# Three output units' rows of x gathered a stage earlier, PSUM tiles split by row half, and mask set-up moved into stage 1

## The chip, the cores and the metric

One core of one Trainium2 chip runs the whole program. The metric is the device time of one execution in microseconds (us), and less is better. Times "before" are the median of three runs. The profile is of one further execution, with a time of its own. In profile lines PE is the tensor engine, PEld its weight load, DVE the vector engine, ACT the scalar engine, POOL the GpSimd engine and SP the sync engine, which here only issues transfers. "SPq" and "POOLq" mark an engine's own issue queue.

## The reference, cut to what matters

Two layers act on x, an array of 512 x 512 positions with 64 channels, in float32. Each adds to x a function of the group-normed x.

```
# layer 0, on xn = layernorm(groupnorm(x)); m = sequence_mask (512 values of 0 or 1)
left  = (xn @ left_w  + left_b)  * m_i * m_j * sigmoid(xn @ lgate_w + lgate_b)
right = (xn @ right_w + right_b) * m_i * m_j * sigmoid(xn @ rgate_w + rgate_b)
out   = einsum('bkjd,bkid->bijd', left, right)            # per channel, sum over k
x1    = x + (layernorm(out) @ out_w + out_b) * sigmoid(xn @ ogate_w + ogate_b)
# layer 1: 12 x 12 low Fourier modes of groupnorm(x1), mixed by complex weights, transformed back
result = x1 + real(ifft2(mixed modes))
```

Rows and columns whose mask is 0 add nothing to `out`. About half of the mask is 1, and when at most 256 (K) of the 512 are, the kernel takes the path `compact`, which packs the masked rows and columns into 256 "slots". That path runs here.

## The kernel before, in words

`compact` is one stream of instructions per engine. Its stages are written out by hand, so each engine works in program order and an instruction that waits holds up everything behind it on its engine.

**Stage 1** (to about 200 us): 16 column blocks `jc` (L677). For each, POOL gathers four tiles of 1 MB from x (`fetch_tile`, L664; the gather itself is L638), PE transposes them (L687), DVE takes statistics of the transposes (`bn_stats`, L688, sixteen per block) and ACT and POOL copy the masked columns of two of the tiles into `xc`, a tile of 257 slots that fills 128.5 KB of each partition (`keep`, L670). After block 8 `make_weights` (L171) scales and centres the weights: short DVE steps, each waiting for a PE product. At the end `group_norm_affine` gives `ab1` (L701), which stage 2 needs.

**Stage 2, the slots' stage** (to about 440 us): iterations q = -14 to 63, one group of four slots each (L773). A group is transposed to channels in place (L719), centred and squared 13 iterations before its use (L727), and its row factors are spread over partitions by way of DRAM in packs of four groups (`spread`, L744: a store `rs_d` and two loads `rbc`, all on POOL's queue, 1 MB together). For q >= 0 `normed` (L759) scales the group, `project` (L764) makes gates and sides in PSUM, ACT takes the sigmoid of the gates into `sigc` (L778), DVE joins both into `o_c` (L795) and SP stores the halves to `left_d` and `right_d` (L807), 512 KB per iteration. From q = 51 on there is no group left to centre, and only the projection half of the loop body runs. `gates_c`, `sides_c` and `sigc` are single buffers that hold both row halves r = 0, 1.

**Between stages 2 and 3** (L813 to L853): broadcast rows of two biases, `center_x` and `gate_x`, the tile `places` (128 KB per partition, used as scratch by everything later), the target indices `dst_i`, and the slots' masks `mask_s` and `mask_own`.

**Stage 3** (to about 621 us): per channel, `left` and `right` are loaded (L865), transposed and multiplied (L895), masked (L900) and stored to `tri_d` (L903).

**Stage 4** (to about 1470 us): a loop over pieces `s` (L1193), eight to a step; 8 steps for the packed product, then 32 for the units of the output, one unit each. The first part makes `u_d`: `load_product` (L1022) brings a product pair into a ring of four buffers, one transfer per partition half; PE multiplies it (L1058), ACT squares and copies (L1078, L1079), DVE reduces and scales (L1083, L1271), POOL adds a bias (L1278) and SP stores `u_d` (L1283). From s = -LEAD on, PE and ACT run 12 to 13 pieces ahead of DVE and POOL. A unit of the output is a pair (column block, half of the rows). `load` (L1091) gathers its two 1 MB tiles of x into one of five ring places of `places`, three units ahead of its use (L1241); so the six gathers of units 0 to 2 stand in the last three steps of the `u_d` part. Then come the gate (L1045), the sigmoid (L1221), the product and the sum with x on POOL (L1109, L1113), statistics and Fourier sums, and the store to `x1_h`.

**Stage 5** (to the end): rows come back from `x1_h`, the inverse transform is added (L1447), and the result is stored (L1448).

Of the kernel before, what the change touches and what calls it, by code (L numbers as in the profile page):

```python
# [9 lines left out]
F32 = mybir.dt.float32  # L10
I32 = mybir.dt.int32
AF = mybir.ActivationFunctionType
ALU = mybir.AluOpType
# [33 lines left out]
def conv_preact_kernel(ctx: ExitStack, tc: tile.TileContext, t: dict):  # L47
# [573 lines left out]
    def compact(fc):  # L621
# [29 lines left out]
            return regs  # L651


        with tc.tile_pool(name="xc", bufs=1) as cp:
            xc = cp.tile([P, K + 1, 2, C], F32, name="xc")
            with tc.tile_pool(name="f1", bufs=1) as sp, tc.tile_pool(name="f1x", bufs=2) as xp, tc.tile_pool(
                name="f1y", bufs=4
            ) as yp, tc.tile_pool(name="f1p", bufs=6, space=PSUM) as pt, tc.manual_schedule():
                make_weights = load_weights(sp, nc.sync)
                sets = chunk_sets(fc, 4, 1)  # L660
                quarter = NJ // 4
                xgs = {}

                def fetch_tile(jc):  # L664
                    xg = xp.tile([P, 2, JC, C], F32, name="xg")
                    xgs[jc] = xg, [xg[:, 0], xg[:, 1]] + [yp.tile([P, JC, C], F32, name="yg") for _ in range(2)]
                    for r, part in enumerate(xgs[jc][1]):
                        gather(part.rearrange("p j c -> p (j c)"), tiles, src_i, r, jc)

                def keep(engine, copy, jc, first, last):  # L670

                    for j, slot in enumerate(slots_of(engine, jc, first, last), first):
                        copy(xc[:, bass.ds(slot, 1)].rearrange("p o r c -> p (o r) c"), xgs[jc][0][:, :, j, :])  # L673

                fetch_tile(0)
                fetch_tile(1)
                for jc in range(NJ):  # L677
                    if jc % quarter == 0:
                        stats = sp.tile([P, 1, 16 * quarter, 6], F32, name="stats1c")
                    for r in range(4):  # L680
                        flat = xgs[jc][1][r].rearrange("p j c -> p (j c)")
                        for c in range(4):

                            ps = pt.tile([P, 4, P], F32, name="x_ps")
                            for i in range(4):
                                o = (8 * c + 2 * i) * C
                                nc.tensor.transpose(ps[:, i, :], flat[:, o : o + P], ident)  # L687
                            nc.vector.bn_stats(  # L688
                                stats[:, 0, 16 * (jc % quarter) + 4 * r + c, :], ps.rearrange("p i k -> p (i k)")
                            )  # L690
# [14 lines left out]
            with tc.tile_pool(name="fn", bufs=2) as np_, tc.tile_pool(name="fw", bufs=2) as wk, tc.tile_pool(  # L705
# [56 lines left out]
                    nc.vector.tensor_mul(xns[q], gts(q), rbs[k][:, n])  # L762

                def project(q, k):  # L764
                    ps = pp.tile([P, 2, N], F32, name=k + "_c")
                    for r in range(2):
                        h = slice(r * C, (r + 1) * C)
                        nc.tensor.matmul(ps[:, r, :], weights[k][h], xns[q][h], start=True, stop=True)
                    return ps


                lead = QB + 9
                for q in range(-lead - 1, groups):  # L773
                    live = lambda i: 0 <= q + i < groups
                    if live(0):
                        gates = project(q, "gates")
                        sig = sp.tile([P, 2, N], F32, name="sigc")
                        nc.scalar.activation(sig, gates, AF.Sigmoid, bias=biases["gates"])  # L778
                    if live(1):
                        normed(q + 1)  # L780
                    for step in todo[:3]:
# [3 lines left out]
                        channels(q + lead + 1)  # L785
                    if live(lead - QB) and (q + lead - QB) % QB == QB - 1:
                        spread((q + lead - QB) // QB)
                    if live(lead):
                        sq, total = centered(q + lead)
                    if live(0):  # L790
# [2 lines left out]
                        res = op.tile([P, 4, 2, P], F32, name="o_c")  # L793
                        for r in range(2):
                            nc.vector.scalar_tensor_tensor(  # L795
                                res[:, :, r, :], sides[:, r].rearrange("p (i k) -> p i k", i=4), biases["sides"],
                                sig[:, r].rearrange("p (i k) -> p i k", i=4), ALU.add, ALU.mult,
                            )
                    if live(lead):
                        nc.vector.tensor_reduce(  # L800
# [9 lines left out]
                            )  # L810


        rows_of = {}  # L813
        with tc.tile_pool(name="rb", bufs=2) as rp, tc.tile_pool(name="rbp", bufs=2, space=PSUM) as rps:
            for name in ("ogate", "out"):
                wide = rp.tile([P, P], F32, name="wide_" + name, tag="wide")
                nc.vector.tensor_copy(wide, biases[name].to_broadcast([P, P]))
                ps = rps.tile([P, C], F32, name="row_" + name, tag="row")
                nc.tensor.matmul(ps, wide, ident[:, :C], start=True, stop=True)
                rows_of[name] = fc.tile([P, C], F32, name="bias_row_" + name)  # L820
                nc.vector.tensor_copy(rows_of[name], ps)
        nc.gpsimd.dma_start(u_d[:, K, 0, :], rows_of["out"])
        nc.gpsimd.dma_start(u_d[:, K, 1, :], rows_of["out"])

        center_x = fc.tile([P, P], F32, name="center_x")
        gate_x = fc.tile([P, P], F32, name="gate_x")
        nc.vector.tensor_scalar(center_x, center, ab1[:, 0:1], None, ALU.mult)
        nc.vector.tensor_scalar(gate_x, weights["ogate"], ab1[:, 0:1], None, ALU.mult)


        with tc.tile_pool(name="tri", bufs=1) as trp:

            places = trp.tile([P, K * 2 * C], F32, name="places")

            dst_i = fc.tile([P, 4, NJ // 2], I32, name="dst_i")
            base = fc.tile([P, 4], F32, name="dst_base")
            nc.vector.tensor_scalar(base, rank_p, float(NJ // 2), None, ALU.mult)
            for b in range(4):
                nc.vector.tensor_scalar(dst_i[:, b, :], few_i, base[:, b : b + 1], None, ALU.add)
            mask_s = fc.tile([P, K], F32, name="mask_s")  # L840
            mask_own = fc.tile([P, 2], F32, name="mask_own")
            with tc.tile_pool(name="mk", bufs=1) as mk, tc.tile_pool(name="mkp", bufs=1, space=PSUM) as mps:
                mask_ps = mps.tile([P, K], F32, name="mask_ps")
                for b in range(2):
                    wide = mk.tile([P, P], F32, name=f"wide{b}")
                    nc.vector.tensor_copy(wide, slot_t[:, b, 1:2].to_broadcast([P, P]))
                    nc.tensor.matmul(mask_ps[:, b * P : (b + 1) * P], wide, ident, start=True, stop=True)
                nc.vector.tensor_copy(mask_s, mask_ps)
                own = mk.tile([P, 2, P], F32, name="own")
                nc.vector.tensor_mul(  # L850
                    own, mask_s.rearrange("p (q b) -> p b q", b=2), ident.unsqueeze(1).to_broadcast([P, 2, P])
                )
                nc.vector.tensor_reduce(mask_own, own, AX.X, ALU.add)  # L853
# [65 lines left out]
            RING = 5  # L919
            first = K * 2 // 64  # L920

            units = [(jc, half) for jc in range(NJ) for half in ((1, 0) if jc < NJ - 1 else (0, 1))]
            total_g = (first + len(units)) * SIZE
            with tc.manual_schedule(), tc.tile_pool(name="late", bufs=1) as lp:
                sets = chunk_sets(lp, 8)
# [9 lines left out]
                sums = lp.tile([P, MODES, M2], F32, name="sums")  # L935
                nc.vector.memset(sums, 0.0)


                order = (0, 1, 3, 4, 2)
# [50 lines left out]
                with tc.tile_pool(name="np_x", bufs=LEAD + 2) as tp, tc.tile_pool(name="np_q", bufs=2) as sqp, tc.tile_pool(  # L990
# [30 lines left out]

                    def load_product(q):  # L1022

                        for h in range(2):
                            nc.sync.dma_start(
                                products_t[q % 4][h * C : (h + 1) * C],
                                tri_d.rearrange("c j i -> c (j i)")[:, (2 * q + h) * 2 * N : (2 * q + h + 1) * 2 * N],
                            )

                    def transpose(s):  # L1030
                        k, n = divmod(s, SIZE)
# [161 lines left out]
                    for s in range(-LEAD, total_g + 2 * SIZE):  # L1193
# [340 lines left out]
```

## Time and profile before

| | us |
|---|---|
| median of 3 runs | 1786.14 |
| lowest and highest run | 1781.57, 1787.03 |
| profiled execution, its own time | 1777.78 |
| span of that execution | 1776.0 |
| PE busy in the span | 1567.8 (88%) |
| DVE busy | 1413.7 (80%) |
| ACT busy | 933.0 (53%) |
| POOL busy | 936.5 (53%) |
| moved by DMA | 518.48 MB |

The span is what the profiler covers; 1.8 us of the execution's time lie around it. The profiled execution was faster than each of the three runs. A line of the timeline has the start in us, the duration, the engine, the program line, the operation, `result<-operands`, sizes and, in brackets, how long the engine had stood idle before it and what ended that. A line of the windows view has the stretch, its length, then busy time and instruction count of PE, PEld, DVE, ACT and POOL, the clock granted to PE (1.00 is full), the mean busy share of the 16 DMA engines and GB/s. A line of the waits view has engine and line, what it waited for, the total in us, how often, and the longest.

### The profile page before, as it was taken

The page shows a single profiled execution, that of the slowest core. Times are in us where ns is not written, and L with a number is a line of the kernel's source. Part 1 is how long each engine was busy: PE and PEld are TensorE (multiplying, and loading weights), DVE is VectorE, ACT ScalarE, POOL GpSimd, SP SyncE. Part 2 cuts the span into 40 slices and gives each one's busy share as a digit, 9 for nine tenths or more (in the row PEclk, how much of TensorE's full clock was granted, in tenths as well). Part 3 has the DMA queues.
Part 4 walks back from the last instruction along what each step waited for, and adds up shares of the span by engine and source line. Part 5 has one row for each costly group of instructions (what it writes and reads, how often), then busy time and mean ns, then how long its engine had stood idle before and what let it go on. Part 6 is the DMA issues. An engine that isn't in the chain of part 4 may idle for free. (4 is left out here: it accounts for less than half of the span.)

```text
span 1776.0 us, 32619 instructions
## 1 busy us (share of the span) xinstructions
PE 1567.8 (88%) x10918; PEld 1242.0 (70%) x10918; DVE 1413.7 (80%) x2982; ACT 933.0 (53%) x1660; POOL 936.5 (53%) x695
## 2 busy tenths in 40 slices
PE   6779799997999978899999999999999977998772
PEld 5667666662899867787888888888888745665341
DVE  7989678887455568688999999999999984865451
ACT  3666566663333266676777777777777742011000
POOL 4666211111000037698999999999999881111110
PEclk9999999999899999899999999999999976555555
DMA  7999278878898789868767767776776699999999
GB/s 281 386 386 388 107 206 227 229 229 245 279 305 303 257 246 347 298 196 296 265 242 257 253 233 259 264 249 239 249 264 244 212 318 400 425 427 427 426 427 385
DMA packets 192593, 518.48 MB, mean 292 GB/s; under 512 B 37664, under 2 KB 104480, under 8 KB 151456
## 3 DMA queue, kind: packets, MB, share of 16 engines
q1 hardware_dynamic: 156112, 295.65, 47.5%
q0 software_dynamic: 32832, 218.45, 33.4%
q10 hardware_dynamic: 3472, 2.20, 0.5%
q8 instruction: 89, 1.46, 0.3%
q14 instruction: 88, 0.72, 0.1%
HBM read 311.60 MB, written 204.60 MB: 291 GB/s over the span
## 5 line engine op out<-in xcount | busy, mean ns | idle before, releaser
L1045 PE MATMUL w_ps<-gate_x,xt_c 128*128 128x128 f32 x2048 | 280.5, 281 | 30.0 <-DVE z_t L1274 28.6
L1113 POOL TENSOR_TENSOR places<-places,z_t 128x1024 f32<-128x1024 f32 x127 | 301.3, 2372 | 8.0
L1045 PEld LDWEIGHTS w_ps<-gate_x,xt_c 128*128 128x128 f32 x2048 | 252.0, 194 | 46.4 <-DVE z_t L1274 44.6
L1045 PE MATMUL c_ps<-center_x,xt_c 128*128 128x128 f32 x2048 | 277.0, 279 | 0.8 <-ACT xt_c L1040 0.4
L1045 PEld LDWEIGHTS c_ps<-center_x,xt_c 128*128 128x128 f32 x2048 | 252.8, 194 | 3.8 <-ACT xt_c L1040 3.0
L1440 PE MATMUL l_ps<-places,rinv 24*128 24x512 f32 x512 | 206.2, 1118 | 29.3 <-DVE places L1447 19.0
L1168 DVE BATCH_NORM_STATS2 stats2c<-places 128x6 f32<-128x128 f32 x1024 | 220.5, 278 | 9.9 <-POOL places L1113 9.9
L1083 DVE TENSOR_REDUCE scratch<-sq_c 128x16 f32<-128x1024 f32 x160 | 194.6, 1216 | 31.1 <-ACT sq_c L1078 16.1
L1221 ACT ACTIVATE z_t<-z_t 128x1024 f32<-128x1024 f32 x128 | 135.5, 1058 | 131.8 <-DVE z_t L1280 131.1
L1440 PEld LDWEIGHTS l_ps<-places,rinv 24*128 24x128 f32 x512 | 119.8, 302 | 110.8 <-DVE places L1447 56.9
L1278 POOL TENSOR_TENSOR z_t<-z_t,bias_row_out 128x1024 f32<-128x1024 f32 x32 | 75.6, 2363 | 226.3 <-PE y_ps L1058 202.1
L1040 ACT ACTIVATE xt_c<-t_ps,ab_xc 128x512 f32<-128x512 f32 x256 | 176.0, 688 | 11.5 <-PE t_ps L1038 10.6
L1274 DVE TENSOR_TENSOR z_t<-w_ps,rs_n 128x512 f32<-128x512 f32 x256 | 172.0, 672 | 6.2 <-PE w_ps L1045 6.1
L1076 ACT ACTIVATE sq_c<-c_ps 128x512 f32<-128x512 f32 x256 | 150.8, 589 | 31.4 <-PE c_ps L1045 30.8
L1280 DVE TENSOR_TENSOR z_t<-z_t,scratch 128x1024 f32<-128x1024 f32 x128 | 156.3, 1221 | 9.9 <-ACT rs_n L1089 3.7
L688 DVE BATCH_NORM_STATS2 stats1c<-x_ps 128x6 f32<-128x512 f32 x256 | 157.1, 682 | 7.7 <-PE x_ps L687 7.4
L1109 POOL TENSOR_TENSOR z_t<-z_t,places 128x1024 f32<-128x1024 f32 x64 | 151.8, 2371 | 14.6 <-ACT z_t L1221 14.4
L1038 PE MATMUL t_ps<-c_ident,places 128*128 128x128 f32 x1024 | 158.4, 278 | 0.0
L1038 PEld LDWEIGHTS t_ps<-c_ident,places 128*128 128x128 f32 x1024 | 118.5, 142 | 51.4 <-issue 51.4
L1447 DVE TENSOR_TENSOR places<-places,l_ps 128x512 f32<-128x512 f32 x176 | 109.3, 682 | 55.2 <-DMA places<-x_h,dst_i 42.1
L1109 POOL TENSOR_TENSOR z_t<-z_t,bias_row_out 128x1024 f32<-128x1024 f32 x63 | 149.4, 2372 | 5.8 <-ACT z_t L1221 5.5
L673 ACT COPY xc<-xg 128x128 f32 x352 | 105.0, 298 | 66.1 <-POOL xc L673 47.1
(214 smaller groups left out, 2557.0 us busy)
## 6 DMA issues: line engine op xcount, KB each, us to landing
x_h<-places SPq DMA_DIRECT2D x64, 1024.0 KB
out_x<-places SPq DMA_DIRECT2D x44, 1024.0 KB
places<-u_d SPq DMA_DIRECT2D x512, 64.0 KB
out_x<-lx_t SPq DMA_DIRECT2D x20, 1024.0 KB
rbc<-rs_d POOLq DMA_DIRECT2D x32, 512.0 KB, 7.1
left_d<-o_c SPq DMA_DIRECT2D x64, 256.0 KB
right_d<-o_c SPq DMA_DIRECT2D x64, 256.0 KB
left_raw<-left_d SPq DMA_DIRECT2D x64, 256.0 KB
```

The source lines that it names most:

```text
L688: nc.vector.bn_stats(stats[:, 0, 16 * (jc % quarter) + 4 * r + c, :], ps.rearrange("p i k -> p (i k)"))
L1038: nc.tensor.transpose(tps[:, i, :], flat[:, o : o + P], ident)
L1040: nc.scalar.activation(xts[s], tps, AF.Identity, bias=ab1[:, 2:3])
L1045: nc.tensor.matmul(ps[:, 2 * i : 2 * i + 2, :], xts[s][:, i, :], w, start=True, stop=True)
L1076: nc.scalar.activation(sq, cps, AF.Square)
L1083: nc.vector.tensor_reduce(totals[k % 2][:, 8 * (n - 1) : 8 * (n + 1)], sqs.pop(s // 2), AX.X, ALU.add)
L1109: nc.gpsimd.tensor_mul(zs[k, c], zs[k, c], u)
L1113: nc.gpsimd.tensor_add(xr, xr, zs.pop((k, c)))
L1168: nc.vector.bn_stats(st[k // 4][:, g, k % 4, :], x_of(k)[:, :, 2 * g : 2 * g + 2])
L1274: nc.vector.tensor_mul(z[:, 8 * odd : 8 * odd + 8, :], wps, rs)
L1280: nc.vector.tensor_add(z, z, bias_ps["ogate"].unsqueeze(1).to_broadcast([P, 16, C]))
L1440: nc.tensor.matmul(ps.rearrange("p j o -> p (j o)"), rinv[h, b, :], it[h], start=True, stop=True, tile_position=(32 * g, 0),)
```

## The change

1. **Early gathers.** `xc` stays allocated after stage 2, and `places` becomes a view of its first 256 slots. In stage 2, at q = 34, 38, ... 54, `early` gathers the six tiles of x of units 0 to 2 into slots whose groups have been projected. Stage 4 starts its own gathers with unit 3.
2. **A PSUM tile per row half.** `project` makes two PSUM tiles, and the sigmoid two SBUF tiles from two activations of half the size. Matmuls and `o_c` steps are as many as before.
3. **Set-up in stage 1.** Bias rows, masks and `dst_i` are made by `prepare_rows` right after `make_weights`, in block 8 of stage 1. Its broadcast and product tiles share one buffer (the tag `scaled`, `bufs=1`). The product for `mask_own` is made in two halves. `center_x` and `gate_x` move into iteration q = -2 of stage 2.
4. **One transfer per product pair.** `load_product` issues one transfer of 128 partitions in place of two of 64.

```diff
+        xc = held.enter_context(tc.tile_pool(name="xc", bufs=1)).tile([P, K + 1, 2, C], F32, name="xc")
+        places = xc.rearrange("p s r c -> p (s r c)")[:, : K * 2 * C]
+        order = (0, 1, 3, 4, 2)
+        EARLY = 3
+        def early(i):
+            k, r = divmod(i, 2)
+            o = (order[k] * 2 + r) * JC * C
+            gather(places[:, o : o + JC * C], tiles, src_i, 2 * units[k][1] + r, units[k][0])
...
+        def prepare_rows(rp):
+            with tc.tile_pool(name="slp", bufs=2, space=PSUM) as rps:
+                for name in ("ogate", "out"):
+                    wide = rp.tile([P, P], F32, name="wide_" + name, tag="scaled")
+                    nc.vector.tensor_copy(wide, biases[name].to_broadcast([P, P]))
+                    ps = rps.tile([P, C], F32, name="row_" + name, tag="row")
+                    nc.tensor.matmul(ps, wide, ident[:, :C], start=True, stop=True)
+                    rows_of[name] = fc.tile([P, C], F32, name="bias_row_" + name)
+                    nc.vector.tensor_copy(rows_of[name], ps)
+                for r in range(2):
+                    nc.gpsimd.dma_start(u_d[:, K, r, :], rows_of["out"])
+                mask_ps = rps.tile([P, K], F32, name="mask_ps", tag="row")
+                for b in range(2):
+                    wide = rp.tile([P, P], F32, name=f"wide{b}", tag="scaled")
+                    nc.vector.tensor_copy(wide, slot_t[:, b, 1:2].to_broadcast([P, P]))
+                    nc.tensor.matmul(mask_ps[:, b * P : (b + 1) * P], wide, ident, start=True, stop=True)
+                nc.vector.tensor_copy(mask_s, mask_ps)
+                for b in range(2):
+                    own = rp.tile([P, P], F32, name=f"own{b}", tag="scaled")
+                    nc.vector.tensor_mul(own, mask_s.rearrange("p (q b) -> p b q", b=2)[:, b], ident)
+                    nc.vector.tensor_reduce(mask_own[:, b : b + 1], own, AX.X, ALU.add)
+                nc.vector.tensor_scalar(base, rank_p, float(NJ // 2), None, ALU.mult)
+                for b in range(4):
+                    nc.vector.tensor_scalar(dst_i[:, b, :], few_i, base[:, b : b + 1], None, ALU.add)
...
                     if jc == NJ // 2:
                         make_weights(fc, cp)
+                        prepare_rows(sp)
...
                 def project(q, k):
-                    ps = pp.tile([P, 2, N], F32, name=k + "_c")
-                    for r in range(2):
+                    made = [pp.tile([P, N], F32, name=f"{k}_c{r}") for r in range(2)]
+                    for r, ps in enumerate(made):
...
-                        sig = sp.tile([P, 2, N], F32, name="sigc")
-                        nc.scalar.activation(sig, gates, AF.Sigmoid, bias=biases["gates"])
+                        sigs = [sp.tile([P, N], F32, name=f"sigc{r}") for r in range(2)]
+                        for sig, ps in zip(sigs, gates):
+                            nc.scalar.activation(sig, ps, AF.Sigmoid, bias=biases["gates"])
...
+                    if q in range(34, 34 + 8 * EARLY, 4):
+                        early((q - 34) // 4)
+                    if q == -2:
+                        nc.vector.tensor_scalar(center_x, center, ab1[:, 0:1], None, ALU.mult)
+                        nc.vector.tensor_scalar(gate_x, weights["ogate"], ab1[:, 0:1], None, ALU.mult)
...
-        with tc.tile_pool(name="rb", bufs=2) as rp, tc.tile_pool(name="rbp", bufs=2, space=PSUM) as rps:
-            for name in ("ogate", "out"):
-                wide = rp.tile([P, P], F32, name="wide_" + name, tag="wide")
...
-            places = trp.tile([P, K * 2 * C], F32, name="places")
...
-                own = mk.tile([P, 2, P], F32, name="own")
...
-                nc.vector.tensor_reduce(mask_own, own, AX.X, ALU.add)
...
                     def load_product(q):
-                        for h in range(2):
-                            nc.sync.dma_start(
-                                products_t[q % 4][h * C : (h + 1) * C],
-                                tri_d.rearrange("c j i -> c (j i)")[:, (2 * q + h) * 2 * N : (2 * q + h + 1) * 2 * N],
-                            )
+                        nc.sync.dma_start(
+                            products_t[q % 4], tri_d.rearrange("c (q h j) i -> q h c (j i)", h=2, j=4)[q]
+                        )
...
-                        if 0 <= v + 3 < len(units):
+                        if EARLY <= v + 3 < len(units):
                             if n == 3:
                                 load(v + 3, 0)
```

More of the change, by code (lines that the diff above doesn't have):

```diff
@@ L651, in slots_of @@
             return regs
-        with tc.tile_pool(name="xc", bufs=1) as cp:
-            xc = cp.tile([P, K + 1, 2, C], F32, name="xc")
+        held = ExitStack()
+        xc = held.enter_context(tc.tile_pool(name="xc", bufs=1)).tile([P, K + 1, 2, C], F32, name="xc")
+        places = xc.rearrange("p s r c -> p (s r c)")[:, : K * 2 * C]
+        units = [(jc, half) for jc in range(NJ) for half in ((1, 0) if jc < NJ - 1 else (0, 1))]
+        order = (0, 1, 3, 4, 2)
[4 more added lines that the diff above has]
+            gather(places[:, o : o + JC * C], tiles, src_i, 2 * units[k][1] + r, units[k][0])
@@ new lines, in compact @@
+        rows_of = {}
+        mask_s = fc.tile([P, K], F32, name="mask_s")
+        mask_own = fc.tile([P, 2], F32, name="mask_own")
+        dst_i = fc.tile([P, 4, NJ // 2], I32, name="dst_i")
+        base = fc.tile([P, 4], F32, name="dst_base")
+        center_x = fc.tile([P, P], F32, name="center_x")
+        gate_x = fc.tile([P, P], F32, name="gate_x")
+        def prepare_rows(rp):
[22 more added lines that the diff above has]
+                    nc.vector.tensor_scalar(dst_i[:, b, :], few_i, base[:, b : b + 1], None, ALU.add)
@@ L656, in compact @@
+        with tc.tile_pool(name="wt", bufs=1) as cp:
             with tc.tile_pool(name="f1", bufs=1) as sp, tc.tile_pool(name="f1x", bufs=2) as xp, tc.tile_pool(
@@ L764, in project @@
                 def project(q, k):
-                    ps = pp.tile([P, 2, N], F32, name=k + "_c")
-                    for r in range(2):
+                    made = [pp.tile([P, N], F32, name=f"{k}_c{r}") for r in range(2)]
+                    for r, ps in enumerate(made):
                         h = slice(r * C, (r + 1) * C)
-                        nc.tensor.matmul(ps[:, r, :], weights[k][h], xns[q][h], start=True, stop=True)
-                    return ps
+                        nc.tensor.matmul(ps, weights[k][h], xns[q][h], start=True, stop=True)
+                    return made
                 lead = QB + 9
@@ L795, in compact @@
                             nc.vector.scalar_tensor_tensor(
-                                res[:, :, r, :], sides[:, r].rearrange("p (i k) -> p i k", i=4), biases["sides"],
-                                sig[:, r].rearrange("p (i k) -> p i k", i=4), ALU.add, ALU.mult,
+                                res[:, :, r, :], sides[r].rearrange("p (i k) -> p i k", i=4), biases["sides"],
+                                sigs[r].rearrange("p (i k) -> p i k", i=4), ALU.add, ALU.mult,
                             )
@@ L810, in compact @@
                             )
-        rows_of = {}
-        with tc.tile_pool(name="rb", bufs=2) as rp, tc.tile_pool(name="rbp", bufs=2, space=PSUM) as rps:
-            for name in ("ogate", "out"):
-                wide = rp.tile([P, P], F32, name="wide_" + name, tag="wide")
[L817 to L831, printed above, removed]
-            places = trp.tile([P, K * 2 * C], F32, name="places")
[L835 to L848, printed above, removed]
-                own = mk.tile([P, 2, P], F32, name="own")
-                nc.vector.tensor_mul(
-                    own, mask_s.rearrange("p (q b) -> p b q", b=2), ident.unsqueeze(1).to_broadcast([P, 2, P])
-                )
-                nc.vector.tensor_reduce(mask_own, own, AX.X, ALU.add)
@@ L854, in compact @@
+        with held:
             with tc.tile_pool(name="ti", bufs=5) as ip, tc.tile_pool(name="tt", bufs=3) as tp, tc.tile_pool(
@@ L920, in compact @@
             first = K * 2 // 64
-            units = [(jc, half) for jc in range(NJ) for half in ((1, 0) if jc < NJ - 1 else (0, 1))]
             total_g = (first + len(units)) * SIZE
@@ L936, in compact @@
                 nc.vector.memset(sums, 0.0)
-                order = (0, 1, 3, 4, 2)
                 def place(i):
@@ L1022, in load_product @@
                     def load_product(q):
-                        for h in range(2):
-                            nc.sync.dma_start(
-                                products_t[q % 4][h * C : (h + 1) * C],
-                                tri_d.rearrange("c j i -> c (j i)")[:, (2 * q + h) * 2 * N : (2 * q + h + 1) * 2 * N],
-                            )
+                        nc.sync.dma_start(
+                            products_t[q % 4], tri_d.rearrange("c (q h j) i -> q h c (j i)", h=2, j=4)[q]
+                        )
                     def transpose(s):
```

## Prediction

> **What bounds the kernel now.** I read the clock and engine shares by stretch first (the windows view), then the waits, then the timeline wherever a stretch had gaps. The chain of waits is of no use here: it begins at 1469 us, behind everything that the change touches, and ends on the final stores. What an edit is worth must be read in its own stage. A change of 0.3% (5.4 us) is about the least that a measurement can tell from none.
>
> Stage 1 ends with DVE. From 126 us to its end it stands still once, for 0.44 us:
>
> ```profile
> 124.66 0.70 DVE L688 BATCH_NORM_STATS2 stats1c<-x_ps 128x6 f32<-128x512 f32 x1 [0.60 <-PE x_ps L687]
> 125.52 0.70 DVE L688 BATCH_NORM_STATS2 stats1c<-x_ps 128x6 f32<-128x512 f32 x1 [0.15 <-PE x_ps L687]
> 126.37 27.60 DVE L688 BATCH_NORM_STATS2 stats1c<-x_ps 128x6 f32<-128x512 f32 x46 [0.16 <-PE x_ps L687]
> ...
> 155.65 35.96 DVE L688 BATCH_NORM_STATS2 stats1c<-x_ps 128x6 f32<-128x512 f32 x60
> 192.05 2.49 DVE L688 BATCH_NORM_STATS2 stats1c<-x_ps 128x6 f32<-128x512 f32 x4 [0.44 <-PE x_ps L687]
> ```
>
> 35.96 us for 60 is 0.60 us each, without a gap. `ab1` follows at 200.3, and ACT waits 7.2 us for it. POOL's last copy of `xc` ends at 196.96, so DVE is late by itself.
>
> Stage 2's main part is bound by PE, its tail (q = 51 to 63) by a loop through two single buffers:
>
> ```profile
> 302.00:316.00 14.00, 14.00 (x85) 8.58 (x83) 12.06 (x28) 9.52 (x14) 1.75 (x3) 1.00 0.82 234
> ```
> ```profile
> 418.80 1.41 DVE L795 SCALAR_TENSOR_TENSOR o_c<-sides_c,b_sides,sigc 128x512 f32<-128x512 f32 x2 [0.77 <-ACT sigc L778]
> 420.12 0.68 DVE L762 TENSOR_TENSOR xnc<-xc,rbc 128x512 f32<-128x512 f32 x1
> ...
> 420.32 1.11 ACT L778 ACTIVATE sigc<-gates_c,b_gates 128x1024 f32<-128x1024 f32 x1 [1.66 <-DVE o_c L795]
> ```
>
> In the first line PE is busy for all 14 us; its rows give 0.96 (gates), 0.49 (transposes), 0.99 (centring) and 0.96 (sides), together the period of 3.40. In the tail `sigc` waits for `o_c`, then `o_c` for `sigc`: 1.41 + 0.11 + 1.11 + 0.15 = 2.78 per iteration, 13 times. Between stages 2 and 3, SP's first load of stage 3 goes out at 444.67, held last by the masks:
>
> ```profile
> SPq L865 <- DVE mask_own L853: 2.8, 1, 2.8
> ```
>
> In stage 4's first part DVE is nearly full (a `total` reduction every 3.0 us), until the gathers of x start at 708.72. Then PE waits for product loads and loses its clock:
>
> ```profile
> 714.83 0.46 PE L1058 MATMUL y_ps<-both,places 64*128 64x128 f32 x2 [0.74 <-DMA places<-tri_d]
> 717.92 0.80 PE L1058 MATMUL y_ps<-both,places 64*128 64x128 f32 x4 [2.64 <-DMA places<-tri_d]
> ```
> ```profile
> 654.00:708.00 54.00, 43.33 (x564) 37.45 (x560) 47.80 (x58) 36.71 (x74) 41.92 (x18) 1.00 1.02 342
> 712.00:716.00 4.00, 2.50 (x32) 2.15 (x32) 3.63 (x6) 2.50 (x5) 3.66 (x4) 1.00 1.03 295
> 716.00:720.00 4.00, 2.08 (x18) 2.08 (x20) 2.24 (x3) 0.00 (x0) 3.72 (x2) 0.63 1.05 354
> 720.00:724.00 4.00, 2.47 (x16) 1.91 (x14) 1.54 (x2) 2.15 (x4) 1.76 (x2) 0.50 0.97 332
> 724.00:728.00 4.00, 3.82 (x24) 3.27 (x26) 0.97 (x2) 1.72 (x3) 2.35 (x1) 0.50 1.02 420
> ```
>
> DMA is full (1.02) before the gathers come on top; DVE falls to a quarter. The L1083 reductions start at 715.73, 722.37, 730.00, 734.04, 737.46, 740.17, 742.87, 746.05: seven steps in 30.3 us, against 21.0 at 3.0 each. The stall costs 9.3 us.
>
> **The change, part by part.**
>
> *Set-up in stage 1: +5.4 us.* In the gap between the stages these DVE steps took 440.18 to 444.54. In stage 1 they stand between `b_out` (ends 124.06) and the next `bn_stats`, on the engine that ends the stage, and one buffer makes them serial. Two rounds of wide copy, product, row copy: the first took 440.18 to 441.46 = 1.28, so about 2.4. Masks: two copies of 0.17, two products at 0.61 (L847: 1.22 for both), latency, one copy of 0.42: 2.2. Four 128x128 steps for `own` at 0.33 (L241, L243): 1.3. `dst_base` and four `dst_i` (L837, L839): 1.0, which before lay in the wait for the first tiles. Sum 6.9, so `bn_stats` restart at 131.0. Before, without their 0.9 us of waits, they would have run as from 125.2. That is 5.8 later, less the 0.44 at 192: +5.4. Bounds: +4 if the rounds overlap as between the stages, +8 if PE, idle longer, feeds DVE slowly and the next gathers (131.97, behind PE's reading) slip too. POOL's two `u_d` stores (0.57 each) fit ahead of its copies at 128.03. `center_x`, `gate_x` (0.28 each) move into iterations in which DVE waits for ACT: 0.
>
> *PSUM and sigmoid split.* Main part: 0, PE stays full with the same matmuls. ACT pays for a second activation: 512-wide forms take 0.59 to 0.77, so two cost 0.1 to 0.4 more than 1.11, on an engine busy 9.5 of 14 us. Tail: half 0's sigmoid can run while DVE joins half 1, so the loop breaks and DVE is next: 0.61 + 2 x 0.66 plus gaps = 2.0 per iteration. 13 x 0.78 = 10 us, if the stores keep up.
>
> *Early gathers, stage 2.* They add 1 MB per four iterations. In the main part the transfers are 82% busy at 234 GB/s; 1 MB at stage 1's 384 GB/s is 2.7 us in 13.7, to about full. `rbc` lands in 7.7 us (median of 300 to 400) and is used five iterations, 17 us, after its pack starts, 2.5 us of which go before its issue: 7 us to spare. On POOL the gather (0.98) stands behind the `rbc` issues; nothing waits behind it for 10 us. No wait of `normed` for a gather is added, since the slots are disjoint. The tail is another matter. From 404.6 it must move 13 x 512 KB of `o_c`, two packs of `rbc` and two gathers: 11.0 MB. At 313 GB/s (stores alone: 15.04 MB at 48% of 100 us) that takes 35 us, at 384 GB/s 29, at stage 4's 342 about 32. So the last store lands near 439 rather than just before 444.67. With the mask wait gone SP loads at once. I take -5 between -9 (DVE sets the pace, 2.0 each, less its wait for `rbc`) and -1 (transfers take 35 us and their landing), the middle rate being that of a stretch at share 1.02.
>
> From 708 to 726 gathers and product loads shared the engines, the gathers' queue at 41% and SP's at 60%, and a gather took 10.0 us to land. The Trainium skill ("DMA: Bandwidth & Descriptors", "Queues, rings and completion order") states a rule behind that row which speaks against this edit: each transfer engine goes round its queues packet by packet, so a gather takes turns with the `o_c` stores. If by the rule the tail gained nothing, the sum would be 5 us higher.
>
> *Stage 4 without six gathers: -9.3*, with 5.9 us of POOL issue time (6 x 0.98). What is late next is DVE at 3.0 us per pair. Bounds: -5 if full DMA alone (share 1.02) keeps the last loads late; -12 if POOL, rid of its gathers, also shortens the following steps. *One load per pair: -0.5*: its second issue (0.55) stood between landing and PE at 624.6; later PE's 0.3 to 0.5 us waits lay beside a full DVE. Bounds 0 and -1.
>
> **Sum**: +5.4 - 5 - 9.3 - 0.5 = **-9.4**. Everything after 755 us moves as a whole, POOL being 91 to 96% busy from 800 to 1400. The profiled time 1777.8 becomes 1768.4. That execution was 8.4 us below the median of the runs, so on the median I forecast **1777** (1786.1 - 9.4).
>
> **Rivals.** *A. Moved, not removed.* Transfers are full in both places: the tail gains 1, the stall halves to -5, stage 1 costs 6: 0, about 1786. For it: shares of 0.82 and 1.02. Against it: from q = 34 to 50, 0.18 of 57 us are free, 10 us, about the 4 x 2.7 of the gathers there. *B. The tail is paced by DVE*: +5 - 9 - 10 = -14, 1772. For it: 425 to 430 moved 302 GB/s at a share of 0.79. *C, slower: late `rbc`.* If gather and stores stretch an `rbc` landing from 7.7 to over 15 us, `normed` waits, and PE with it. The price is read at 717.92: a gap of 2.64 us and 12 us at half clock, in which a stage bound by PE loses 6. Two such stops give +17: -9.4 + 17 = +8, 1794. It decides from the second stop on. For it: one `rbc` already came 1.38 us late at 427.14; gathers beside full queues took 10.0 us. *D. The split changes nothing*, as `o_c` still waits in the old order: the tail gains 1 for the masks alone, -5, 1781.
>
> The skill's "TensorE: Matmul & The Clock Gate", "What's actually happening", has full clock back after some 3.4 us of activity; the trace shows 0.63, 0.50, 0.50 and then 0.66 to 732, after only 2.64 us of idling. By the rule C would cost 9 us rather than 17, and still end near no change; I go by the trace.
>
> **Chances.** Forecast (-6 to -12) 0.52, B 0.15, A and D within 5.4 us 0.19, C 0.14. Faster 0.67, same 0.19, slower 0.14. The range takes in the bounds: lowest 4 - 9 - 13 = -18, highest 8 - 1 - 5 = +2 and a little of C: **1768 to 1789**.
>
> **What would show it.** Right: `ab1` 4 to 8 us later; the tail at 2.0 to 2.5 per iteration; first `left_raw` load not waiting for DVE; no PE wait over 1 us for `tri_d`, clock 1.00, around 715; everything from unit 0 on some 9 us earlier. Wrong: `xnc` waiting for `rbc` before 400, half clock in stage 2, or a PE stop before the first `t_ps`.

## The result, and the profile after

| | before | changed kernel |
|---|---|---|
| median of 6 runs, us | 1784.22 | 2032.87 |
| lowest and highest run | 1781.54, 1787.03 | 2030.53, 2036.45 |
| ratio, 95% interval | | 1.1397 [1.1379, 1.1415] |
| span of the profiled execution, us | 1776.0 | 2031.2 |
| moved by DMA, MB | 518.48 | 518.47 |

The kernel became 14% slower where 0.5% faster was forecast. The same bytes are moved, so the place to look is where the transfers go slowly. The page of the changed kernel has it in its rows of 40 slices (50.8 us each): DMA's share, GB/s and PE's clock all collapse from slice 13 to 20, which is the product loop of stage 4.

```profile
PEclk9989899989997556555799999999999997555555
DMA  8988378888993122222377678677677769999999
GB/s 297 384 343 322 80 235 236 282 292 301 302 305 120 53 89 98 90 98 89 127 247 272 232 249 294 214 260 254 237 236 248 277 219 316 411 425 427 427 427 394
```

Its list of costly groups names the wait. The last column is idle time of PE ahead of the product matmuls, all of it for the product load; in the profile of before this wait was 18.2 us.

```profile
L1067 PE MATMUL y_ps<-both,xc 64*128 64x128 f32 x1024 | 120.6, 425 | 235.5 <-DMA xc<-tri_d 235.5
```

`xc<-tri_d` is `load_product`: the ring of product buffers lies in `xc` now, so the name of the tile is new and the transfer is the one of part 4. The windows view of two stretches of the same loop, and after it the transfers from 650 to 700 us:

```profile
650.00:700.00 50.00, 18.93 (x160) 17.60 (x160) 7.01 (x7) 12.22 (x22) 0.00 (x0) 0.61 0.13 53
700.00:750.00 50.00, 18.92 (x160) 17.60 (x160) 12.37 (x16) 10.95 (x21) 11.69 (x5) 0.50 0.22 90
```
```profile
DMA packets 655, 2.65 MB, mean 53 GB/s; under 512 B 10, under 2 KB 10, under 8 KB 654
...
q1 hardware_dynamic: 654, 2.64, 12.8%
...
xc<-tri_d SPq DMA_DIRECT2D x7, 512.0 KB
```

From 650 to 700 us nothing but product loads is on its way, and they take 12.8% of the sixteen engines' time, as much as 2.05 engines have. The packet records of the trace say the same: from 652 to 690 us two packets of this queue are on their way at almost every moment, each of 4 KB and 0.157 us, where before there were mostly 16. PE asks for the next pair all the time and gets one in 9.94 us, where before a pair took 3.0:

```profile
693.97 3.78 PE L1067 MATMUL y_ps<-both,xc 64*128 64x128 f32 x32 [6.14 <-DMA xc<-tri_d]
703.91 3.78 PE L1067 MATMUL y_ps<-both,xc 64*128 64x128 f32 x32 [6.16 <-DMA xc<-tri_d]
713.85 3.78 PE L1067 MATMUL y_ps<-both,xc 64*128 64x128 f32 x32 [6.16 <-DMA xc<-tri_d]
```

The rest answers to the lines shown of before. In stage 1 the set-up takes DVE from 126.56 to 133.65; in stage 2's main part PE is full as it was (14.00 of 14.00); in the tail DVE waits twice for `rbc`, and after the second wait once more, for the sigmoid, while PE's clock is low (0.50 from 440 to 444 us); and SP's first `left_raw` load waits for its own stores, no longer for the masks.

```profile
126.56 0.22 DVE L680 COPY wide_ogate<-b_ogate 128x128 f32<-128x128 f32 x1
...
133.06 0.67 DVE L699 TENSOR_SCALAR dst_i<-few_i,dst_base 128x8 int32<-128x8 f32 x4
133.65 2.48 DVE L734 BATCH_NORM_STATS2 stats1c<-x_ps 128x6 f32<-128x512 f32 x4
```
```profile
312.00:326.00 14.00, 14.00 (x85) 8.46 (x83) 11.97 (x26) 10.25 (x18) 1.75 (x3) 1.00 0.80 247
```
```profile
419.88 1.41 DVE L848 SCALAR_TENSOR_TENSOR o_c<-sides_c,b_sides,sigc 128x512 f32<-128x512 f32 x2
421.20 0.68 DVE L809 TENSOR_TENSOR xnc<-xc,rbc 128x512 f32<-128x512 f32 x1
422.06 1.41 DVE L848 SCALAR_TENSOR_TENSOR o_c<-sides_c,b_sides,sigc 128x512 f32<-128x512 f32 x2 [0.17 <-ACT sigc L826]
426.92 0.69 DVE L809 TENSOR_TENSOR xnc<-xc,rbc 128x512 f32<-128x512 f32 x1 [3.45 <-DMA rbc<-rs_d]
...
440.22 0.69 DVE L809 TENSOR_TENSOR xnc<-xc,rbc 128x512 f32<-128x512 f32 x1 [3.55 <-DMA rbc<-rs_d]
...
444.91 1.41 DVE L848 SCALAR_TENSOR_TENSOR o_c<-sides_c,b_sides,sigc 128x512 f32<-128x512 f32 x2 [2.07 <-ACT sigc L826]
```
```profile
SPq L879 <- DMA left_d<-o_c: 1.7, 1, 1.7
```

The first product load goes out at 631.5, 10.4 us later than before (621.1); the first `u_d` tile is asked for at 1011.6 in place of 759.7. So 241 of the 252 us come about between those two points.

### The profile page after: what moved, and what is told of

Same layout as the page of the kernel before. It is cut to its first block, busy times and chain, and to the rows that moved or that the text cites. A ratio compares the mean times of both kernels' runs of the same rounds, so it can differ in the third digit from the quotient of the medians.

```text
span 2031.2 us, 32680 instructions
## 1 busy us (share of the span) xinstructions
PE 1616.1 (80%) x10918; PEld 1290.8 (64%) x10918; DVE 1413.7 (70%) x2984; ACT 948.1 (47%) x1724; POOL 936.0 (46%) x695
## 2 busy tenths in 40 slices
DMA packets 191634, 518.47 MB, mean 255 GB/s; under 512 B 36704, under 2 KB 103520, under 8 KB 150496
## 5 line engine op out<-in xcount | busy, mean ns | idle before, releaser
L1067 PE MATMUL y_ps<-both,xc 64*128 64x128 f32 x1024 | 120.6, 425 | 235.5 <-DMA xc<-tri_d 235.5
L1122 POOL TENSOR_TENSOR xc<-xc,z_t 128x1024 f32<-128x1024 f32 x127 | 301.2, 2372 | 8.0
L1067 PEld LDWEIGHTS y_ps<-both,xc 64*128 64x128 f32 x1024 | 112.4, 326 | 243.9 <-issue 243.6
L1449 PE MATMUL l_ps<-xc,rinv 24*128 24x512 f32 x512 | 208.5, 1124 | 31.1 <-DVE xc L1456 18.8
L1177 DVE BATCH_NORM_STATS2 stats2c<-xc 128x6 f32<-128x128 f32 x1024 | 220.5, 278 | 8.8 <-POOL xc L1122 8.8
L1449 PEld LDWEIGHTS l_ps<-xc,rinv 24*128 24x128 f32 x512 | 120.4, 304 | 114.3 <-DVE xc L1456 59.8
L1087 ACT ACTIVATE sq_c<-y_ps 128x512 f32<-128x512 f32 x64 | 38.2, 597 | 290.5 <-PE y_ps L1067 290.5
L734 DVE BATCH_NORM_STATS2 stats1c<-x_ps 128x6 f32<-128x512 f32 x256 | 155.8, 680 | 11.2 <-PE x_ps L733 9.3
L1118 POOL TENSOR_TENSOR z_t<-z_t,xc 128x1024 f32<-128x1024 f32 x64 | 151.6, 2369 | 15.0 <-ACT z_t L1230 14.9
L1047 PE MATMUL t_ps<-c_ident,xc 128*128 128x128 f32 x1024 | 158.2, 277 | 0.0
```

Source lines behind the costliest of these rows:

```text
L734: nc.vector.bn_stats(stats[:, 0, 16 * (jc % quarter) + 4 * r + c, :], ps.rearrange("p i k -> p (i k)"))
L1047: nc.tensor.transpose(tps[:, i, :], flat[:, o : o + P], ident)
L1067: nc.tensor.matmul(ps[:, h, i, :], of[hs, i, :], both[hs], start=True, stop=True)
L1118: nc.gpsimd.tensor_mul(zs[k, c], zs[k, c], u)
L1122: nc.gpsimd.tensor_add(xr, xr, zs.pop((k, c)))
L1177: nc.vector.bn_stats(st[k // 4][:, g, k % 4, :], x_of(k)[:, :, 2 * g : 2 * g + 2])
```

## The experiments

**Theories.** Theory 1: the merged load reads `tri_d` through the pattern `q h c (j i)`, whose slowest dimension is h = 2, and a transfer is shared out over as many engines as that dimension can fill: two. Each of the former half loads had 64 rows there. Theory 2: one transfer of 128 partitions is slow as such. Theory 3: not the load, but what lies around it: x gathered into `xc`, and the product ring in the same tile.

The Trainium skill ("DMA: Bandwidth & Descriptors", "Why a DMA increments its semaphore by 16 and not by 1") states that the number of engines is the largest number up to 16 that divides the slowest dimension of both patterns, leaving out dimensions of size 1. That is Theory 1 as a rule. Its "Rules for kernel authors" also say that two transfers to disjoint halves of the partitions gain nothing over one of 128, which is Theory 1's opposite if the pattern is not looked at. The first four runs decide between them.

**1. Two loads again, the rest of the change kept.**

```diff
-                        nc.sync.dma_start(
-                            products_t[q % 4], tri_d.rearrange("c (q h j) i -> q h c (j i)", h=2, j=4)[q]
-                        )
+                        for h in range(2):
+                            nc.sync.dma_start(products_t[q % 4][h * C : (h + 1) * C], ...)
```

> The changed kernel with part 4 undone: a product pair is loaded by two transfers of 64 partitions again. Theory 1 (the merged load's source has only two entries in its slowest dimension, and so runs on two of the sixteen DMA engines): stage 4's stall of some 250 us is gone, the time is 1775 to 1788, and PE waits for product loads under 10 us in all. The lower end if the other steps of the prediction hold (1777), the upper if the trace of the changed kernel is right that the product loop's first load goes out 10 us late (631.5 against 621.1) against 9 us won from the stall. Theory 2 (a transfer of 128 partitions is slow in itself): the same time, no help here. Theory 3 (x gathered into the slots' tile, or the product ring lying in it, holds stage 4 up): stays near 2033.

Measured: 1778.84 us (before 1783.32), ratio 0.9975 [0.996, 0.999]. 254 us are gone with this one edit, so they were part 4's, and Theory 3 in its plain form falls with them: this kernel has its tiles and gathers in place. PE's wait for product loads is 13.0 us, a little over the 10 expected; 6.6 of it is the first load's landing.

**2. The kernel before, with part 4 alone.**

> The kernel before with part 4 alone: one transfer of 128 partitions per product pair. Theories 1 and 2: 32 loads at about 10 us each in place of a loop at 3.0 us per pair, so 2010 to 2040, with 50 to 60 GB/s where only product loads run. Theory 3: 1780 to 1790, as before.

Measured: 2036.49 us, ratio 1.1425 [1.1385, 1.1465]; +253 us by one edit. Its profile has the same rate where only product loads run:

```profile
DMA packets 524, 2.13 MB, mean 53 GB/s; under 512 B 8, under 2 KB 8, under 8 KB 522
...
q1 hardware_dynamic: 522, 2.11, 12.8%
```

Theory 3 is out. Theories 1 and 2 are left.

**3. One load of 128 partitions, its source in 16 groups; 4. the same in 4 groups.** `tri_d` is laid out by product pairs, as G groups of 128 / G rows with one unused row behind each group, so that the slowest dimension cannot be joined to the next. Only G differs.

```diff
-        tri_d = dram.tile([C, K, K], F32, name="tri_d")
+        tri_d = dram.tile([K // 8, G, 128 // G + 1, 4 * K], F32, name="tri_d")
...
+                    rows = tri_d.rearrange("q (h g) r (s n) -> (q h) g r s n", h=2, s=2)
+                    nc.sync.dma_start(rows[:, c // (128 // G), c % (128 // G)], out_t)
...
+                        nc.sync.dma_start(products_t[q % 4], tri_d[q, :, : 128 // G])
```

> The changed kernel with one transfer of 128 partitions per product pair, but tri_d laid out by pairs, 16 groups of 8 rows with an unused row behind each, so that the source's slowest dimension has 16 entries; bytes and pieces (4 KB) as in the merged load. Theory 1: all sixteen engines, so the same as with two loads within 3 us, 1772 to 1788. Theory 2: stays near 2033. Theory 3: stays near 2033.

> The same layout with 4 groups of 32 rows, so that the slowest dimension has 4 entries. Theory 1: four engines, twice the 53 GB/s that two moved, so 106 GB/s and 4.95 us for 512 KB; against the 3.0 us per pair of the loop 32 x 1.95 = 62 us over the kernel with 16 groups, 1835 to 1860 (more if PE loses its clock in the waits). Theory 2: near 2033. Theory 3: near 2033.

Measured: 16 groups 1781.33 us, ratio 0.9991 [0.9974, 1.0008]; 4 groups 1874.73 us, ratio 1.0512 [1.048, 1.0544]. One transfer is not slow as such, which ends Theory 2; and the number of rows in the slowest dimension sets the rate, as Theory 1 has it: 53 GB/s with two, 106 with four, and in the packet records two and four packets at a time. The transfers view of the kernel with 4 groups, from 650 to 690 us, shows twice the rate of two in the slices in which only product loads run:

```profile
DMA  2222222222223222222222222239322494222294
GB/s 107 106 106 106 98 107 106 106 106 106 107 98 123 106 106 107 106 106 102 102 107 106 106 106 106 102 147 422 139 106 107 164 410 156 98 107 107 123 414 172
```

Four groups cost 93 us over sixteen, where 62 were expected. The rate was right (pairs start at 651.61, 656.61, 661.58, 666.56: 4.98 us each), but once `u_d` is stored beside the loads a pair takes 6.2 us; in the changed kernel 9.94 becomes 11.19. The difference is about 1.25 us in both. The three slices with a share of 9 and over 400 GB/s are such stores, which take nearly all sixteen engines. A store of 512 KB that is shared out evenly over 16 engines puts 32 KB on each, and at 53 / 2 = 26.5 GB/s an engine needs 1.24 us for that. The two numbers agree, and so the likely reason is that a load held to few engines also waits for what else those engines carry. With the measured periods, 9 pairs at 9.94 and 22 at 11.19 make 335.6 us from the first pair to the last; the trace has 336.1 (644.25 to 980.38).

**5 to 8. The other steps, one at a time,** from the kernel with two loads (1778.84, ratio 0.9975). Run 5 moves rows and masks from block 8 of stage 1 into stage 2's ramp, and `dst_i` ahead of stage 1; run 6 sets `EARLY = 0`; run 7 takes the split back; run 8 shifts the early gathers.

```diff
-                        prepare_rows(sp)
...
+                    if q in range(-12, -4, 2):
+                        prepare_rows((q + 12) // 2, sp, pp)
```

> From the kernel with two loads (1778.84): rows and masks are made in iterations -12 to -6 of stage 2, where DVE waits for ACT more than half of the time, and dst_i ahead of stage 1. If the set-up steps are on the path in stage 1, bn_stats restart 7 us earlier after b_out and the time is 1770 to 1774. Rival: stage 1 has slack elsewhere (PE idle and its clock low around the set-up, gathers behind it), or the ramp only shifts the cost: 1777 to 1780.

Measured: 1773.60, ratio 0.9938 [0.9922, 0.9953]. The set-up cost stage 1 between 5.2 us (medians) and 6.6 us (ratios); in the ramp no cost of it can be seen in these times.

```diff
-        EARLY = 3
+        EARLY = 0
```

> From the kernel with two loads: the six gathers of units 0 to 2 back in stage 4, nothing else changed. If moving them is worth the stall (9.3) and costs the slots' stage nothing: 1786 to 1790. If their place in the tail costs it the two waits for rbc of 3.5 us each that the changed kernel's trace shows: 1779 to 1783, with no rbc wait over 1.5 us in the tail and a stall at the product loop's end. Rival C of the prediction (the late rbc costs more than the stall saves): under 1777.

Measured: 1788.92, ratio 1.0028 [1.0019, 1.0037]. The early gathers are worth 10 us, all that was hoped. The traces give the two sides of it: from the first product matmul to the first `u_d` load 137.0 us without them, 123.6 with them; and from `ab1` to the first `left_raw` load 242.6 without, 245.7 with. So in these two executions 13.4 are won and 3.1 paid. The tail of stage 2 waits for `rbc` without them too (once, 4.78 us), so the gathers are not the only cause of that wait.

```diff
-                    made = [pp.tile([P, N], F32, name=f"{k}_c{r}") for r in range(2)]
+                    ps = pp.tile([P, 2, N], F32, name=k + "_c")
...
-                        sigs = [sp.tile([P, N], F32, name=f"sigc{r}") for r in range(2)]
+                        sig = sp.tile([P, 2, N], F32, name="sigc")
```

> From the kernel with two loads: one PSUM tile and one sigmoid per iteration again. If the split takes 10 us off the tail (2.78 to 2.0 per iteration): 1785 to 1789. If the tail waits for transfers in either form (rival D): 1777 to 1780. A gain from leaving it out (one activation of 1.11 us in place of two of 0.7) would show as under 1776.

Measured: 1780.22, ratio 0.9978 [0.9967, 0.9989]: no difference that these runs can tell. The split's gain in the tail is lost again.

```diff
-                    if q in range(34, 34 + 8 * EARLY, 4):
-                        early((q - 34) // 4)
+                    if q in range(16, 16 + 8 * EARLY, 4):
+                        early((q - 16) // 4)
```

> From the kernel with two loads: the six gathers stand at iterations 16, 20, ... 36 in place of 34, 38, ... 54, all in the main part of stage 2, where the transfers are 82% busy. If the tail's two waits of 3.5 us for rbc come from the two gathers there, they go, and the time is 1769 to 1775. Rival: in the main part the same gathers delay rbc (17 us in use, 7 to spare by the prediction's working), PE stops there and loses its clock: 1780 to 1795.

Measured: 1779.03, ratio 0.9971 [0.9956, 0.9986]: no difference. One of the tail's two waits for `rbc` went, and the other grew to 5.71 us. Main part: `normed` waited 4.1 us for `rbc` in all, far less than the rival's price.

**9 to 11. Why the split gave nothing.** In the tail an iteration takes 2.1 us in place of 3.4, so the last packs of `rbc` are needed sooner, while a pack cannot start before one of two buffers is free, and its loads wait for the store of 16 KB ahead of them (`rs_d`) to land. For the last pack of the changed kernel it was the store, not the buffer: the group that frees the buffer was scaled at 421.20, the store went out at 422.50, and the loads at 431.58. Run 9 gives `rbc` a third buffer and brings the last pack forward (its factors too, five steps per iteration in place of three), on top of runs 5 and 8; run 10 is run 9 without the split; run 11 is run 9 with the gathers where the change had them.

```diff
-                    rbs[k] = np_.tile([P, QB, N], F32, name="rbc")
+                    rbs[k] = spare.tile([P, QB, N], F32, name="rbc")
...
-                    for step in todo[:3]:
+                    some = 5 if q + lead >= groups else 3
+                    for step in todo[:some]:
...
+                    if q == groups - lead + 1:
+                        spread(groups // QB - 1)
```

> Set-up in the ramp and the gathers at iterations 16 to 36 (both from the earlier runs), and besides a third buffer for rbc and the last pack's factors and spread two iterations earlier. If the tail's gain from the split is lost to the last packs of rbc, which come late because their buffer and their place in the order hold them, the wait for rbc in the tail (5.7 and 7.8 us in all in the kernels without this) falls under 2 us, and the time is 1765 to 1770, against 1773.6 of the kernel with set-up in the ramp alone. Rival: the transfers themselves bound the tail (busy 93 to 97% there), and the wait only moves to another pack or to the stores: 1771 to 1776.

> The same without the split of PSUM tile and sigmoid (tail at 2.78 per iteration). If with rbc in time the split is worth what the prediction gave it (0.78 us in 13 iterations, 10 us, less what DVE and the transfers take): 6 to 10 us above the kernel with the split. If the transfers bound the tail in either form (rival D): within 2 us of it.

> As the first of these three, but with the gathers at iterations 34 to 54, where the change put them. If two gathers in the tail cost transfer time there (2 MB at about 380 GB/s, 5.5 us): 3 to 6 us above the first. If main part and tail have the same room for them: within 2 us.

Measured: run 9 1770.47, ratio 0.9927 [0.9914, 0.994]; run 10 1774.71, 0.9954 [0.9941, 0.9968]; run 11 1777.00, 0.997 [0.996, 0.9981]. Run 9 lies 0.5 us outside its expected range and is the fastest kernel here. The waits view of its DVE from 400 to 460 us, and four steps of its timeline, show the tail near the pace that the prediction had worked out for the split (2.10 us per iteration, 2.0 forecast), with `rbc` in time:

```profile
DVE xnc L823 <- DMA rbc<-rs_d: 0.5, 1, 0.5
```
```profile
433.89 1.41 DVE L867 SCALAR_TENSOR_TENSOR o_c<-sides_c,b_sides,sigc 128x512 f32<-128x512 f32 x2
...
436.00 1.41 DVE L867 SCALAR_TENSOR_TENSOR o_c<-sides_c,b_sides,sigc 128x512 f32<-128x512 f32 x2
...
438.09 1.41 DVE L867 SCALAR_TENSOR_TENSOR o_c<-sides_c,b_sides,sigc 128x512 f32<-128x512 f32 x2
...
440.19 1.41 DVE L867 SCALAR_TENSOR_TENSOR o_c<-sides_c,b_sides,sigc 128x512 f32<-128x512 f32 x2
```

Whether the third buffer or the earlier pack did this was not taken apart. Run 10 goes at 2.78 again and loses 4 to 5 us, less than the 6 to 10 expected, but more than the 2 of the rival. Run 11 bears on what held `rbc`. These are POOL's issues in run 11, then in run 9, for the last pack:

```profile
412.87 1.02 POOL L638 DMA_INDIRECT xc<-in_x,src_i  x1 [0.30 <-issue]
413.89 0.53 POOL L812 DMA_DIRECT2D rs_d<-turned_c  x1
425.39 1.25 POOL L816 DMA_DIRECT2D rbc<-rs_d  x2 [10.97 <-DVE o_c L867]
```
```profile
417.06 0.52 POOL L812 DMA_DIRECT2D rs_d<-turned_c  x1 [3.33 <-ACT turned_c L810]
422.77 1.23 POOL L816 DMA_DIRECT2D rbc<-rs_d  x2 [5.18 <-DVE o_c L867]
```

In run 11 the small store stands right behind a 1 MB gather on POOL's queue, and POOL goes on to the loads 11.5 us after issuing it; in run 9, without a gather ahead of it, 5.7 us after. The releaser that the lines name (`o_c`) is the event that came last by the profile and not what is waited for: the loads read what the store writes. In runs 1 and 6 the waits view of 400 to 460 us names the store itself; in run 1 a gather was issued 2.7 us ahead of it (420.00 and 422.74), in run 6 there is none:

```profile
POOL rbc L802 <- DMA rs_d<-turned_c: 8.4, 1, 8.4
```
```profile
POOL rbc L802 <- DMA rs_d<-turned_c: 8.7, 2, 4.9
```

So the store lands late where a gather stands ahead of it (8.4 us against 4.9 at most). The changed kernel shows it in the main part too: there the loads go out 3.1 and 3.5 us behind their store ahead of the first gather, and 6.6 to 7.2 us behind it afterwards. Whether that comes from its place in the queue, or from the gather's 1 MB on engines that are full anyhow (97% busy from 400 to 440 us in run 11, 89 to 93% in run 9), was not separated. Run 11 is 6.5 us above run 9, a little over the 3 to 6 expected, and 3.4 above run 5 (5.7 by the ratios), which has two buffers and the last pack in its old place: there the store went out 3.1 us behind the gather (416.34 against 413.24), here 1.0. Bringing the pack forward helped only where no gather stood ahead of it.

## Why the prediction was wrong, point by point

**One load per pair: -0.5, "bounds 0 and -1". This step failed.** The prediction priced the second issue (0.55 us) that goes away and never asked at what rate the merged transfer runs; the bound "0" said that one transfer can't be worse than two. It costs +254 us (run 1 against the changed kernel), +253 by itself (run 2): 9.9 to 11.2 us per pair at the rate of two engines, 32 times, against 3.0. The row that should have raised the question was in the trace of before, which had the transfers full in this very loop (a share of 1.02 at 342 GB/s): there, a load's rate is the price, not its issue. And the diff shows the pattern, `q h c (j i)` with h=2 in front. None of the rivals held this case, so the whole range missed.

**Set-up in stage 1: +5.4 (bounds +4 and +8). Right.** DVE took 7.1 us where 6.9 was worked out, and taking it out again wins 5.2 to 6.6. The profiles of before and after alone would have misled: the step behind the last statistics of stage 1 starts 9.6 us later in the second (204.19 against 194.57). But in run 2, whose stage 1 is that of before, it starts at 198.66, and in run 5, without the set-up there, at 198.09. So about 4 us of the 9.6 are the spread of single executions, and some 5.5 are left for the set-up.

**PSUM and sigmoid split with the masks' wait: -5 (bounds -9 and -1). Mis-sized, within its bounds**, at rival D's end: the split gives 0.5 to 1.4 us (run 7), and what the three parts give together in run 1 (-4.5) leaves nothing for the masks either. In the traces, from `ab1` to the first `left_raw` load, split and masks without the gathers (run 6) save 1.9 us: 242.6 against 244.5 before. D's reason, that `o_c` still waits in the old order, is not what happened: in the changed kernel's tail most iterations run at 2.0 to 2.6 us. The others are the two with the waits for `rbc` (5.5 and 5.6) and one behind each (3.1 and 4.1), where PE's clock was down (0.66 from 428 to 432 us, 0.50 from 440 to 444). What the loop gains is handed to these. The prediction gave `rbc` 7 us to spare, out of 17 us for five iterations of the main part; at the tail's 2.1 us five iterations are 10.5. Where `rbc` is in time the split is worth 4 to 5 us (run 9 against run 10).

**Early gathers: 0 in the main part, and -9.3 in stage 4. Right in sum**: 10 us (run 6), but by luck in part, since it is 13.4 less 3.1 in the traces: more than the bound of 12 in stage 4, less a price in stage 2 that this term did not have. The sentence that nothing waits behind the gather on POOL for 10 us is false. In the changed kernel the next `rs_d` store came 8.7 us behind the first gather and 4.9 to 5.5 behind the others of the main part, where the slack took the delay; in the tail it came 3.1 us behind, and the slack was gone. Rival C had this wait and the loss of PE's clock with it, priced for a stage that PE bounds. Both came, in the tail: from 420 to 440 us PE's clock is 0.84 in runs 5 and 11 and 1.00 in run 9, and in the changed kernel it cost the iterations just named.

**The sum without the failed step.** -9.4 + 0.5 = -8.9 was forecast for the three other parts; run 1 measures 0.25% of 1784, that is -4.5 (interval -1.8 to -7.1). The difference lies in the tail, whose term gave about 1 of its 5 us.

## What to carry to other kernels

When two transfers become one, read the new access pattern before counting issues: the size of its outermost dimension has to fill the engines. Here two rows there held 512 KB, in pieces of 4 KB, to 53 GB/s and four rows to 106. Put partitions, or rows laid out for the purpose, outermost. And a stage that is made faster needs its inputs sooner: a small store that others wait for is better not issued right behind a large gather.

## What the runs showed that was not expected

- One engine moved some 26.5 GB/s (53 for two, 105 to 107 for four), in pieces of 4 KB; two carried 512 KB in 9.9 us.
- A load on few engines was held up by other transfers: about +1.25 us per 512 KB store, with two engines and with four, though with two the sixteen were idle for 78% of the time (share 0.22).
- PE working 3.78 us in each 9.94 us stayed at about half its clock for hundreds of microseconds (0.50 from 700 to 750, 0.57 from 800 to 900), which made its own work on a pair longer (3.78 us) than a pair's whole period before (3.0 us).
- With its slowest dimension full, one load per pair was no better than two (1781.33 [ratio 0.9974 to 1.0008] against 1778.84 [0.996 to 0.999]): no gain of part 4 was seen. (The layout of `tri_d`, and so its stores, differ between these two.)
